# RWKV scan on one core: values repeated by DMA instead of by TensorE, and the outer mix product in four row groups

## The chip, the cores and the metric

The kernel runs on one core of one Trainium2 chip. A core has TensorE (PE, matmuls, with weight loads PEld beside them), VectorE (DVE), ScalarE (ACT), GpSimd (POOL) and SyncE (SP, which here only issues DMAs). Matmuls write to PSUM; everything else lives in SBUF, and DMA engines move data between SBUF and DRAM. The metric is device time in microseconds, the median of some runs. Before the change it is 3527.54 us (3 runs, 3523.34 to 3530.71).

## The reference

Four layers run one after the other on x of shape (16, 100, 512): a cross-attention (layer 0), an RWKV block (layer 1), a second cross-attention with a feed-forward part (layer 2), and another RWKV block (layer 3). The change touches the two RWKV blocks alone. Their core, with 32 heads of 16 channels:

```python
xa = _ln(x, ln1_w, ln1_b)
sx = jnp.concatenate([state[:, 1:2] - xa[:, :1], xa[:, :-1] - xa[:, 1:]], axis=1)
xxx = jnp.tanh((xa + sx * maa_x) @ maa_w1).reshape(b, l, 5, DM)
xxx = jnp.einsum('blfd,fde->blfe', xxx, maa_w2)
xm = xa[:, :, None] + sx[:, :, None] * (maa_stack + xxx)
xk, xw, xv, xr, xg = (xm[:, :, j] for j in range(5))
w = jnp.exp(-jnp.exp(time_decay + jnp.tanh(xw @ td_w1) @ td_w2)).reshape(b, l, h, s_)
r, k, v = (...)   # xr @ Wr.T, xk @ Wk.T, xv @ Wv.T
g = jax.nn.silu(xg @ Wg.T)
def step(s, rkvw):
    r_t, k_t, v_t, w_t = rkvw
    a = k_t[..., :, None] * v_t[..., None, :]
    out = jnp.einsum('bhi,bhij->bhj', r_t, u * a + s)
    s = a + w_t[..., :, None] * s
    return (s, out)
```

For each head the state is a 16 x 16 matrix: every key channel i meets every value channel j. Behind the recurrence stand a group norm, the gate, the product with Wo, and a channel mix with three more 512 x 512 products (Wfk, Wfr, Wfv). The mix product is the second einsum: five mixes f, each a product over only DM = 32 hidden channels into 512 output channels.

## The kernel before

The 16 sequences are worked in 4 groups g of 4 (T = 400 columns: 4 sequences of 100 steps), and the 512 channels in 4 chunks c of 128. A chunk C = 4g + c holds 8 heads, that is 8 x 256 pairs (i, j), which lie on 128 partitions x 2 rows in 8 *units*. An RWKV layer has 16 chunks and so 128 units; the loop at L1231 runs over them, from u = -42 (group 0's projections come first, with no units) to a tail behind unit 127. DVE, ACT, POOL and PE instructions that go through the wrappers at L69 and L81 keep the order in which the program writes them (their line in the profile is L77 or L82); SP's DMAs do not go through a wrapper.

What one slot u of the loop writes (L1251 to L1274):

- `spread(u + 1)`: two matmuls of 32 rows each, one for each row of a unit's row pair, with a 0/1 matrix `sel`, repeat the value rows of the chunk (`vc`) over 128 partitions into a PSUM tile `vb` (two of them in turn, two banks each), shifted by one step; ACT copies the start state from `s0r` into each sequence's first column.
- `product(u)`: DVE multiplies `vb` by the repeated keys `kr`, in place, 128 x 792.
- what was put off to this slot: readers of PSUM banks of the slot before (`slots.begin()`), among them `tm` on DVE and `xj` on POOL for the mixes.
- `scan(u)`: two DVE scans (128 x 400 each) over the decay `wr` and `vb`, into an SBUF tile `a` (4 of them); then POOL multiplies `a` by the repeated receptance `rr`, in place.
- `enter`, `repeat`, `bonus`, `gates` at fixed slots of a chunk: DMAs on SP that load a chunk's v, k, r (`vc`, `kc`, `rc`) and the repeated `kr`, `wr`, `rr` (one tile for two rows; four DMAs each, one for a quarter of the partitions) from DRAM, where `store` put them from ACT's queue.
- `gather` in odd slots: PE sums the finished units u-3 and u-2 over i into the PSUM bank `acc`; after a chunk's last one comes `norm`.
- then *pieces*: projections of the next group, the product with Wo, the channel mix. Each has a price in us, and a slot takes pieces until a budget is used up: 2.5 in units 0 to 28, 2.95 up to unit 95, 3.9 from unit 96 on, less what gather and bonus take.

The mix product is `mixed(f, c)`, twenty pieces of 0.67 in a group, each one matmul of 32 rows into a bank of its own; three banks `mm0` to `mm2` serve all pieces. Every group: 2 inner products (`inner`), then mixes, keys (`plain` with Wk), decay, values, receptance and gate in the order written out at L945 to L969.

The core of a unit, in the code:

```python
vector.tensor_tensor_scan(
    a[:, i, :], rep["w"][:, i, :], vbs[u % 2][:, i, :T], 0.0, ALU.mult, ALU.add
)
gpsimd.tensor_tensor(a, a, rep["r"], ALU.mult)
```

Of the kernel before, what the change touches and what calls it, by code (L numbers as in the profile page):

```python
# [9 lines left out]
F32 = mybir.dt.float32  # L10
# [7 lines left out]
G = 4  # L18
# [17 lines left out]
def xattn_sequence(ctx: ExitStack, tc: tile.TileContext, d: dict, out: bass.AP):  # L36
# [42 lines left out]
    vector, scalar, gpsimd = InOrder(nc.vector), InOrder(nc.scalar), InOrder(nc.gpsimd)  # L79
# [80 lines left out]
    class Slots:  # L160
# [22 lines left out]
        def read_later(self, bank, fn):  # L183
            once = self.readers[id(bank)] = self.defer(1, fn)
            return once
# [450 lines left out]
    def rwkv(n, ws, next_weights, last):  # L636
# [6 lines left out]
        with ExitStack() as es:  # L643
# [6 lines left out]
            vbs = [psum.tile([128, 2, 512], F32, name=f"vb{i}") for i in range(2)]  # L650
            acc = psum.tile([128, 512], F32, name="acc")
            slots = Slots([psum.tile([128, 512], F32, name=f"mm{i}") for i in range(3)])
# [3 lines left out]
            w2a = one.tile([128, E], F32, name="maa_w2a")  # L656
            nc.sync.dma_start(out=w2a, in_=d[f"L{n}_maa_w2"][0:128, :])

            w2b = one.tile([96, E], F32, name="td_maa_w2")
            nc.sync.dma_start(out=w2b[:64], in_=d[f"L{n}_td_w2"])  # L660
            nc.sync.dma_start(out=w2b[64:], in_=d[f"L{n}_maa_w2"][128:160, :])
# [27 lines left out]
            fold = one.tile([128, 32], F32, name="fold")  # L689
            nc.vector.tensor_reduce(fold, ident.rearrange("p (r s) -> p s r", s=32), AX.X, ALU.add)  # L690
            sel = one.tile([128, 16, 32], F32, name="sel")
            for j in range(16):
                nc.vector.tensor_copy(
                    sel[:, j, :].rearrange("p (h i) -> p h i", i=16),
                    fold.rearrange("p (h j) -> p h j", j=16)[:, :, j : j + 1].to_broadcast([128, 2, 16]),
                )


            share = one.tile([128, 2], F32, name="share")
            nc.vector.tensor_reduce(share, heads8.rearrange("p (q h) -> p h q", h=2), AX.X, ALU.add)  # L700
# [3 lines left out]
            for jg in range(4):  # L704
                nc.vector.tensor_copy(
                    gat[:, jg, :].rearrange("p (h g q) -> p g q h", g=4, q=4)[:, jg],
                    heads8.rearrange("p (q h) -> p q h", h=2),
                )
                nc.vector.tensor_tensor(
                    gat[:, jg, :].rearrange("p (h j) -> p h j", j=16),  # L710
                    gat[:, jg, :].rearrange("p (h j) -> p h j", j=16),
                    share[:, :, None].to_broadcast([128, 2, 16]), ALU.add,
                )

            s0r = one.tile([128, 4, NC, 4, B], F32, name="s0r")
            for r in range(4):
                rs = slice(32 * r, 32 * r + 32)
                ps = slots.bank()
                for c in range(NC):
                    for jq in range(4):  # L720
                        mm(
                            out=ps[32 * jq : 32 * jq + 32, c * 64 : (c + 1) * 64], lhsT=ident[rs, rs],
                            rhs=s0[rs, c].rearrange("p b (g q) -> p q g b", q=4)[:, jq],
                            start=True, stop=True,
                        )
# [72 lines left out]

            def projections(g, base):
                nm = f"{n}_{g}"  # L800
                to = put[g] = {
                    t: dram.tile([NC, 4, 32, T], F32, tag=t, name=f"d{t}_{nm}")
                    for t in ("k", "v", "r", "w", "g")
                }

                def store(t, c, tile):
                    nc.scalar.dma_start(out=to[t][c].rearrange("r p t -> (r p) t"), in_=tile)
# [48 lines left out]
                def inner(lo, hi):  # L856
                    p0, z = (0, "z0") if lo == 0 else (64, "tz")
                    rs = slice(p0, p0 + hi - lo)
                    chain(
                        2.7, late, None, soon, lambda ps: ps[rs, :T], lambda c: w1[:, c, lo:hi],  # L860
                        lambda c: st["xm"][:, c, :],
                        lambda ps: scalar.activation(st[z][rs, :], ps[rs, :T], AF.Tanh),
                    )

                def mixed(f, c):

                    if c == 0:
                        xj[f] = two.tile([128, NC, T], F32, tag="xm", bufs=3, name=f"xj_{nm}_{f}")
                    ps = slots.bank()
                    cols = slice(c * 128, (c + 1) * 128)  # L870
                    rs = slice(32 * f, 32 * f + 32) if f < 4 else slice(64, 96)
                    w, z = (w2a, st["z0"]) if f < 4 else (w2b, st["tz"])
                    mm(out=ps[:, :T], lhsT=w[rs, cols], rhs=z[rs, :], start=True, stop=True)

                    def read():
# [6 lines left out]
                    mixes[f].append(slots.read_later(ps, read))  # L882
# [61 lines left out]
                mix = lambda f, c: piece(0.67, lambda: mixed(f, c), late)  # L944
                inner(0, 128)  # L945
                mix(0, 0)
                inner(128, 160)
                for c in range(1, NC):
                    mix(0, c)
                mix(1, 0)  # L950
                mix(1, 1)
                plain(0, "Wk", "k", 0)
                plain(0, "Wk", "k", 1)
                mix(1, 2)
                plain(0, "Wk", "k", 2)
                mix(1, 3)
                plain(0, "Wk", "k", 3)
                mix(2, 0)
                decay_in()
                for c in range(NC):  # L960
                    if c:
                        mix(2, c)
                    piece(0.67, lambda c=c: decay(c), late)
                for f, w, t in ((2, "Wv", "v"), (3, "Wr", "r")):
                    for c in range(NC):
                        mix(f + 1, c)
# [4 lines left out]
            def channels(g, slot):  # L971
# [41 lines left out]
                def keys(co):  # L1013
                    def read(ps):
                        if co == 0:
                            st["kk"] = two.tile([128, NC, T], F32, tag="kk", bufs=1, name=f"kk_{nm}")
# [19 lines left out]
                def values(i):  # L1036
                    b = g * G + i

                    def read(ps):
                        def add():  # L1040
# [3 lines left out]
                            if last:  # L1044
                                nc.sync.dma_start(out=out[b], in_=xb[b])
# [43 lines left out]
            def enter(C):  # L1089
# [4 lines left out]
                for k, bufs in (("v", 2), ("k", 1), ("r", 1)):  # L1094
                    t[k] = two.tile([128, T], F32, tag=f"{k}c", bufs=bufs, name=f"{k}c_{n}_{C}")
                    nc.sync.dma_start(out=t[k], in_=put[g][k][c].rearrange("r p t -> (r p) t"))
                repeat(C, 0)

            def repeat(C, rp):
                g, c = C // NC, C % NC  # L1100
                rep = chunks[C]["rep"][rp] = {}
                for t in ("k", "w", "r"):
                    rep[t] = two.tile([128, 2, T], F32, tag=f"{t}rep", bufs=3, name=f"{t}r_{n}_{C}_{rp}")
                    for jq in range(4):
                        nc.sync.dma_start(
                            out=rep[t][32 * jq : 32 * jq + 32],
                            in_=put[g][t][c, 2 * rp : 2 * rp + 2].rearrange("r p t -> p r t"),
                        )
# [23 lines left out]
            def spread(u):  # L1132

                C, jg, rp = where(u)
                p4 = vbs[u % 2][:, :, :T].rearrange("p r (b t) -> p r b t", t=L)
                for i in range(2):
                    rs = slice(64 * rp + 32 * i, 64 * rp + 32 * i + 32)
                    mm(
                        out=p4[:, i, :, 1:L], lhsT=sel[rs, 4 * jg : 4 * jg + 4, :].rearrange("p q m -> p (q m)"),
                        rhs=steps(chunks[C]["v"][rs, :])[:, :, 0 : L - 1], start=True, stop=True,  # L1140
                    )
                g = C // NC
                scalar.copy(
                    p4[:, :, :, 0], s0r[:, 2 * rp : 2 * rp + 2, C % NC, jg, g * G : (g + 1) * G]
# [577 lines left out]
```

## Time and profile before

| | us |
|---|---|
| median of 3 runs | 3527.54 |
| the profiled execution | 3530.07 |
| its span, first to last instruction | 3528.3 |
| layer 1: units 0 to 28 | 859 to 987 |
| layer 1: units 29 to 63 | 987 to 1147 |
| layer 1: units 64 to 95 | 1147 to 1313 |
| layer 1: units 96 to 127 | 1313 to 1499 and a little on |
| layer 3: the same four | 2785, 2913, 3072, 3238, 3425 |
| spread on PE (`vb<-vc,sel`), both layers | 261.0 |
| mix product on PE (`mm<-z,maa_w2a`, f under 4), both layers | 120.2 |
| POOL's `a<-a,rr`, 256 times | 480.9 |
| DVE's scans, 512 times | 475.7 |
| DVE's product, 256 times | 250.5 |

Busy time is the union of a group's instructions[...]. A float32 matmul stands in the profile as two records. The share of the TensorE clock that was granted is 0.935 over the span. Idle time of an engine that does not set the pace costs nothing. DMAs are issued from SP (queue q1) and ACT (q10).

### The profile page before, as it was taken

How to read it: one execution, taken by the hardware profiler on the slowest of the kernel's cores; microseconds unless marked ns; L12 is line 12 of the kernel's file. 1: busy time of each engine (PE TensorE's matmuls, PEld its weight loads, DVE VectorE, ACT ScalarE, POOL GpSimd, SP SyncE). 2: the span in 40 equal slices, each digit the busy share in tenths (PEclk: the TensorE clock that was granted, in tenths of full speed). 3: DMA queues.
4: the chain of work that ended last, by engine and by line, in shares of the span. 5: the costliest groups of instructions: out<-in, count | busy, mean ns of one | idle time of the engine just before them, and what ended most of it. 6: DMA issues, size and time to landing. Idle time of an engine off the chain costs nothing. (4 is left out here: it accounts for less than half of the span.)

```text
span 3528.3 us, 46276 instructions
## 1 busy us (share of the span) xinstructions
PE 3217.1 (91%) x17795; PEld 1432.9 (41%) x17795; DVE 1770.8 (50%) x3570; ACT 981.8 (28%) x1715; POOL 1376.4 (39%) x1036
## 2 busy tenths in 40 slices
PE   6899998868999988988999999789998899998898
PEld 3444443333333333334454555345553333333333
DVE  4777777723777665514333333310001477775651
ACT  1322223222233233321322223211112233333232
POOL 1444444443666665511212111210002466665551
PEclk8999999978999989999999999999997899998998
DMA  5000001012434441101000010110012243433310
GB/s 169 21 31 21 31 21 33 1 56 86 126 108 124 126 146 54 38 27 55 25 19 19 19 31 18 39 53 8 10 57 68 87 129 104 134 115 117 87 29 14
DMA packets 153426, 216.60 MB, mean 61 GB/s; under 512 B 23498, under 2 KB 132106, under 8 KB 153206
## 3 DMA queue, kind: packets, MB, share of 16 engines
q1 hardware_dynamic: 130166, 180.87, 17.3%
q10 hardware_dynamic: 23040, 32.78, 2.6%
q8 instruction: 140, 2.29, 0.3%
q14 instruction: 80, 0.66, 0.1%
HBM read 174.25 MB, written 36.04 MB: 60 GB/s over the span
## 5 line engine op out<-in xcount | busy, mean ns | idle before, releaser
L77 POOL TENSOR_TENSOR a<-a,rr 128x800 f32<-128x800 f32 x256 | 480.9, 1879 | 342.4 <-DVE a L77 269.7
L77 DVE TENSOR_TENSOR_SCAN a<-wr,vb 128x400 f32<-128x400 f32 x512 | 475.7, 971 | 19.8 <-PE acc L82 10.9
L77 DVE TENSOR_TENSOR vb<-vb,kr 128x792 f32<-128x792 f32 x256 | 250.5, 979 | 197.0 <-ACT vb L77 195.5
L77 DVE CUSTOM_DVE_ANT_0 junk<-l_sc,mask 100x361 f32<-100x361 f32 x512 | 273.0, 533 | 90.1 <-PE l_sc L82 73.6
L82 PE MATMUL vb<-vc,sel 32*128 32x396 f32 x1024 | 261.0, 568 | 3.4 <-DVE a L77 2.2
L77 DVE TENSOR_TENSOR pt<-l_sc,maskT 121x400 f32<-121x400 f32 x384 | 193.5, 566 | 89.9 <-PE l_sc L82 89.0
L77 ACT ACTIVATE pt<-pt 121x1600 f32<-121x1600 f32 x96 | 147.6, 1538 | 282.2 <-DVE pt L77 280.7
L1425 DVE CUSTOM_DVE_ANT_0 junk<-l2a_sc,mask 100x361 f32<-100x361 f32 x256 | 136.9, 535 | 172.9 <-PE l2a_sc L82 155.7
L77 POOL TENSOR_TENSOR xj<-tm,ext 128x400 f32<-128x400 f32 x160 | 152.8, 962 | 174.3 <-DVE tm L77 168.0
L77 DVE SCALAR_TENSOR_TENSOR tm<-mm,vec,sx 128x400 f32<-128x400 f32 x160 | 99.9, 631 | 235.6 <-PE mm L82 190.9
L1461 POOL TENSOR_TENSOR pa<-pt,pt 121x1600 f32<-121x1600 f32 x16 | 57.2, 3574 | 366.8 <-ACT pt L1456 366.8
L63 PE MATMUL h<-yTb,l_fc 128*128 128x400 f32 x512 | 175.3, 505 | 8.2 <-ACT yTb L229 8.2
L1642 DVE TENSOR_TENSOR x<-pb,x 100x512 f32<-100x512 f32 x16 | 12.8, 799 | 338.3 <-DMA pb<-po 332.7
L82 PE MATMUL v<-l_v_w,ct 128*121 128x512 f32 x384 | 180.0, 613 | 0.0
L82 PE MATMUL k<-ct,l_k_w 128*128 128x361 f32 x512 | 173.0, 481 | 7.3 <-DVE mv_l2a L207 7.3
L77 POOL TENSOR_TENSOR pa<-pt,pt 121x1600 f32<-121x1600 f32 x32 | 114.7, 3586 | 165.5 <-ACT pt L77 165.5
L63 PE MATMUL p<-l_proj,h 128*128 128x512 f32 x384 | 165.4, 592 | 0.0
L77 ACT COPY vb<-s0r 128x8 f32<-128x8 f32 x256 | 43.0, 168 | 408.7 <-PE vb L82 322.9
L82 PE MATMUL l_sc<-kz,qz 32*100 32x361 f32 x1024 | 117.1, 528 | 42.6 <-DVE pt L77 21.7
L82 PEld LDWEIGHTS vb<-vc,sel 32*128 32x128 f32 x1024 | 84.8, 190 | 146.9 <-issue 107.3
L82 PE MATMUL mm<-l_Wo,gc 128*100 128x512 f32 x256 | 124.6, 629 | 8.4 <-POOL gc L77 8.4
L63 PEld LDWEIGHTS h<-yTb,l_fc 128*128 128x128 f32 x512 | 98.1, 192 | 83.3 <-ACT yTb L229 10.1
(258 smaller groups left out, 5305.6 us busy)
## 6 DMA issues: line engine op xcount, KB each, us to landing
kr<-dk SPq DMA_DIRECT2D x256, 100.0 KB
wr<-dw SPq DMA_DIRECT2D x256, 100.0 KB
rr<-dr SPq DMA_DIRECT2D x256, 100.0 KB
ct<-in_ctxT SPq DMA_DIRECT2D x32, 722.0 KB
dk<-k ACTq DMA_DIRECT2D x32, 200.0 KB
kc<-dk SPq DMA_DIRECT2D x32, 200.0 KB
dw<-wd ACTq DMA_DIRECT2D x32, 200.0 KB
dv<-v ACTq DMA_DIRECT2D x32, 200.0 KB
```

What stands on the lines that cost most here:

```text
L63: nc.tensor.matmul(out=ps, lhsT=lhs(c), rhs=rhs(c), start=(c == 0), stop=(c == n - 1))
L77: return lambda *args, **kw: tc.keep_in_program_order(op(*args, **kw))
L82: pin(nc.tensor.matmul(**kw))
L1425: nc.vector.tensor_tensor_reduce(out=junk, in0=ss[r][:L, :S2], in1=t["mask"], scale=-1.0, scalar=FLT_MAX, op0=ALU.add, op1=ALU.min, accum_ ...
L1461: nc.gpsimd.tensor_tensor(t["pa"], t["pt"][0], pt, ALU.add)
L1642: nc.vector.tensor_tensor(x, pb[:, i, :], x, ALU.add)
```

## The change

Values are no longer spread by PE. The stores of k, v, r and w in DRAM get another order (channel by channel, so that the four rows of a partition stand beside each other), the values one element further on, with a small number in front, so that a read from the element before gives the values shifted by one step. `fetch(u)` then brings a unit's values, repeated, straight into its tile `a` (now 6 tiles), with two DMAs of 64 partitions, two slots ahead. ACT writes the first column there (`first`), product and scans work in place in `a`. The repeats of k, w and r become one DMA of 128 partitions each, spread over more slots, and the stores and the loads of v, k and r become four DMAs each. The matrices `gat`, `fold` follow the new order of the partitions. SP's DMAs in this part are now kept in program order too.

The PSUM of `vb` goes to the pieces, which have seven banks instead of three. `hidden(f)` copies the 32 rows of a mix's hidden channels to all four quarters of the partitions (four DMAs on SP), the weights `w2a` lie by chunks in the four quarters, and `mixed(f)` writes the four chunks' matmuls one after the other, each in its own rows of PE and its own bank. It is one piece of 0.75. Its readers come one slot later for c = 0, 1 and two for c = 2, 3. The order of the pieces is written anew. The budgets stay. Further, the weights of the channel mix are loaded in quarters over slots 82 to 96 instead of at once in slot 93, and the tile `kk` shares its buffers with the mixes.

```diff
-            vbs = [psum.tile([128, 2, 512], F32, name=f"vb{i}") for i in range(2)]
-            slots = Slots([psum.tile([128, 512], F32, name=f"mm{i}") for i in range(3)])
+            slots = Slots([psum.tile([128, 512], F32, name=f"mm{i}") for i in range(7)])
...
-            w2a = one.tile([128, E], F32, name="maa_w2a")
-            nc.sync.dma_start(out=w2a, in_=d[f"L{n}_maa_w2"][0:128, :])
+            w2a = one.tile([128, 5, 128], F32, name="maa_w2a")
+            for c in range(NC):
+                nc.sync.dma_start(
+                    out=w2a[32 * c : 32 * c + 32],
+                    in_=d[f"L{n}_maa_w2"][:, c * 128 : (c + 1) * 128].rearrange("(f k) m -> k f m", k=32),
+                )
...
                 def store(t, c, tile):
-                    nc.scalar.dma_start(out=to[t][c].rearrange("r p t -> (r p) t"), in_=tile)
+                    for ps, rows in rows_of(g, t, c):
+                        nc.scalar.dma_start(out=rows, in_=tile[ps])
...
+                def hidden(f):
+                    z = st["z0"][32 * f : 32 * f + 32, :] if f < 4 else st["tz"][64:96, :]
+                    t = st["zr", f] = two.tile([128, T], F32, tag="zr", bufs=2, name=f"zr_{nm}_{f}")
+                    for c in range(NC):
+                        sync.dma_start(out=t[32 * c : 32 * c + 32, :], in_=z)
+                def mixed(f):
+                    xj[f] = two.tile([128, NC, T], F32, tag="xm", bufs=3, name=f"xj_{nm}_{f}")
+                    banks = [slots.bank() for c in range(NC)]
+                    for c, ps in enumerate(banks):
+                        rs = slice(32 * c, 32 * c + 32)
+                        mm(out=ps[:, :T], lhsT=w2a[rs, f, :], rhs=st["zr", f][rs, :], start=True, stop=True)
+                    if f < 4:
+                        hidden(f + 1)
...
+                    for c, ps in enumerate(banks):
+                        mixes[f].append(slots.read_later(ps, lambda c=c: read(c), 1 + c // 2))
...
                 inner(0, 128)
-                mix(0, 0)
                 inner(128, 160)
+                mix(0)
+                plain(0, "Wk", "k", 0)
+                mix(1)
...
-            def spread(u):
+            def fetch(u):
                 C, jg, rp = where(u)
-                p4 = vbs[u % 2][:, :, :T].rearrange("p r (b t) -> p r b t", t=L)
-                for i in range(2):
-                    rs = slice(64 * rp + 32 * i, 64 * rp + 32 * i + 32)
-                    mm(
-                        out=p4[:, i, :, 1:L], lhsT=sel[rs, 4 * jg : 4 * jg + 4, :].rearrange("p q m -> p (q m)"),
-                        rhs=steps(chunks[C]["v"][rs, :])[:, :, 0 : L - 1], start=True, stop=True,
-                    )
+                g, c = C // NC, C % NC
+                a = products[u] = two.tile([128, 2, T], F32, tag="a", bufs=6, name=f"a_{n}_{u}")
+                v = put[g]["v"]
+                for h in range(2):
+                    n0 = v.offset + (c * 128 + 64 * h + 16 * jg + 2 * rp) * T
+                    sync.dma_start(
+                        out=a[64 * h : 64 * h + 64],
+                        in_=bass.AP(v.tensor, n0, [[0, 16], [4 * T, 4], [1, 2 * T]]),
+                    )
+            def first(u):
...
                 scalar.copy(
-                    p4[:, :, :, 0], s0r[:, 2 * rp : 2 * rp + 2, C % NC, jg, g * G : (g + 1) * G]
+                    products[u].rearrange("p r (b t) -> p r b t", t=L)[:, :, :, 0],
+                    s0r[:, 2 * rp : 2 * rp + 2, C % NC, jg, g * G : (g + 1) * G],
                 )
...
             def product(u):
                 C, jg, rp = where(u)
-                p4 = vbs[u % 2][:, :, :T].rearrange("p r (b t) -> p r b t", t=L)
+                p4 = products[u].rearrange("p r (b t) -> p r b t", t=L)
...
-                a = products[u] = two.tile([128, 2, T], F32, tag="a", bufs=4, name=f"a_{n}_{u}")
+                a = products[u]
                 for i in range(2):
-                    vector.tensor_tensor_scan(
-                        a[:, i, :], rep["w"][:, i, :], vbs[u % 2][:, i, :T], 0.0, ALU.mult, ALU.add
-                    )
+                    vector.tensor_tensor_scan(a[:, i, :], rep["w"][:, i, :], a[:, i, :], 0.0, ALU.mult, ALU.add)
                 gpsimd.tensor_tensor(a, a, rep["r"], ALU.mult)
...
                     rep[t] = two.tile([128, 2, T], F32, tag=f"{t}rep", bufs=3, name=f"{t}r_{n}_{C}_{rp}")
-                    for jq in range(4):
-                        nc.sync.dma_start(
-                            out=rep[t][32 * jq : 32 * jq + 32],
-                            in_=put[g][t][c, 2 * rp : 2 * rp + 2].rearrange("r p t -> p r t"),
-                        )
+                    x = put[g][t]
+                    n0 = x.offset + (c * 128 + 2 * rp) * T
+                    sync.dma_start(
+                        out=rep[t], in_=bass.AP(x.tensor, n0, [[4 * T, 32], [0, 4], [1, 2 * T]])
+                    )
...
-                if u == UNITS - 32 - 3:
-                    cm.update(load(n, "Wfk", "Wfr", "Wfv"))
+                for k, at_u in (("Wfk", UNITS - 46), ("Wfr", UNITS - 40), ("Wfv", UNITS - 35)):
+                    if 0 <= u - at_u < NC:
+                        load_part(cm, n, k, u - at_u)
...
+                if 0 <= u + 2 < UNITS:
+                    fetch(u + 2)
                 if 0 <= u + 1 < UNITS:
-                    spread(u + 1)
+                    first(u + 1)
```

## The prediction

> **What bounds the kernel now.** The page's first part says that TensorE is 91% busy and that no other engine passes 50%. That is an average, so I went on to the busy time by stage. The product instruction of a unit (one slice of the RWKV recurrence) writes `vb` once; its start times in the timeline cut each RWKV layer into units. The stretches below hold layer 1's units 0-29, 29-64, 64-96 and 96-127 (layer 3 repeats them within 1 us; the two layers' units are 1280 of 3528 us). Columns: length, then busy us (instructions) of PE, weight load, DVE, ACT, POOL, then granted clock, DMA share, GB/s.
> ```profile
> PE 3217.1 (91%) x17795; PEld 1432.9 (41%) x17795; DVE 1770.8 (50%) x3570; ACT 981.8 (28%) x1715; POOL 1376.4 (39%) x1036
> ...
> 859.00:987.00 128.00, 125.43 (x460) 47.67 (x458) 97.41 (x121) 36.60 (x83) 86.11 (x70) 0.92 0.35 103
> 987.00:1147.00 160.00, 152.29 (x596) 58.22 (x596) 118.01 (x148) 57.40 (x118) 106.53 (x86) 0.94 0.39 115
> 1147.00:1313.00 166.00, 149.80 (x557) 56.91 (x557) 110.01 (x137) 54.86 (x110) 110.16 (x94) 0.90 0.45 136
> 1313.00:1499.00 186.00, 173.76 (x594) 63.26 (x592) 110.45 (x133) 64.68 (x127) 98.27 (x79) 0.92 0.18 51
> ```
> A unit lasts 128/29 = 4.41, 4.57, 5.19 and 6.00 us, and TensorE fills 90 to 98% of it. DVE and POOL have room, but only as long as they may run at the same time: their busy times add up to 183.5 us in a stretch of 128. So the next question is what lets them overlap. The groups and the per-tile views show whom:
> ```profile
> L77 POOL TENSOR_TENSOR a<-a,rr x256: 1861/1878/1901, 869.2 to 3431.3; 128x800 f32<-128x800 f32 x128
> ...
> L77 DVE TENSOR_TENSOR_SCAN a<-wr,vb x512: 954/969/989, 867.3 to 3430.1; 128x400 f32<-128x400 f32 x171
> L77 DVE TENSOR_TENSOR vb<-vb,kr x256: 958/980/992, 859.4 to 3424.5; 128x792 f32<-128x792 f32 x128
> ...
> L77 DVE SCALAR_TENSOR_TENSOR th_1b<-th_1b,mm x16: 653/689/689, 1340.6 to 1597.3; 100x512 f32<-100x512 f32 x16
> L77 DVE SCALAR_TENSOR_TENSOR x<-th_1b,x x16: 691/692/1650, 1341.4 to 1598.0; 100x512 f32<-100x512 f32 x16
> ...
> L1642 DVE TENSOR_TENSOR x<-pb,x x16: 691/693/1751, 2369.1 to 2668.5; 100x512 f32<-100x512 f32 x16
> ```
> (Three numbers: shortest/median/longest ns.) The product and the scans each read one operand from PSUM (`vb`), and neither they nor POOL's multiplication ever stretch, though they run beside each other all the time. The two DVE instructions with both inputs in SBUF, `x<-th_1b,x` and `x<-pb,x`, take 0.69 us or up to 1.75. The timeline shows when they stretch:
> ```profile
> 1438.80 0.69 DVE L77 SCALAR_TENSOR_TENSOR th_1b<-th_1b,mm 100x512 f32<-100x512 f32 x1 [1.61 <-PE mm L82]
> 1439.53 1.30 DVE L77 SCALAR_TENSOR_TENSOR x<-th_1b,x 100x512 f32<-100x512 f32 x1
> ...
> 1439.25 1.04 POOL L77 TENSOR_TENSOR og<-og,sq 128x400 f32<-128x400 f32 x1 [0.89 <-ACT sq L77]
> ...
> 1470.23 1.88 POOL L77 TENSOR_TENSOR a<-a,rr 128x800 f32<-128x800 f32 x1
> 1470.28 0.69 DVE L77 SCALAR_TENSOR_TENSOR th_1b<-th_1b,mm 100x512 f32<-100x512 f32 x1 [2.56 <-PE mm L82]
> 1471.01 1.65 DVE L77 SCALAR_TENSOR_TENSOR x<-th_1b,x 100x512 f32<-100x512 f32 x1
> ```
> POOL's `og` ends at 1440.29 and the DVE instruction at 1440.83; POOL's `a` ends at 1472.11, DVE at 1472.66: each time 0.55 us later, its 0.69 without a start-up. It stood still until POOL was done. `th_1b<-th_1b,mm`, same length, one operand in PSUM, ran through the same POOL instruction in 0.69. The reverse shows too: a `gc` multiplication that POOL started at 1351.85 behind a DVE instruction of two SBUF inputs took 1.48 us, not 1.03, and ended 0.89 after it.
>
> [...] The trace agrees in every such pair of full length (above; beside `rstd`, of 4 elements, nothing stretched). No scan with two SBUF inputs is in it[...]. [...] layer 0's `l_sc<-qz,kz` (768 records, two a matmul, four row groups in turn) has 92.8 us, 0.24 a matmul, against 120.2/128 = 0.94 for the mix product's `mm<-z,maa_w2a`.
>
> **The change, part by part** (profiled execution: 3530.07 us, span 3528.28).
>
> 1. *Spread removed from PE.* 512 matmuls, 261.0 us of PE over both layers: 1.02 us of each unit. A gain only where PE stays the bound.
> 2. *Mix product side by side.* 20 matmuls a group become 5 bursts: 20 x 0.87 to 0.94 less 5 x 0.97, some 13 us of PE a group, 0.4 a unit. In group 0's lead-in (745-859, no scans, PE 94.6 of 114 busy) this lies on the path; against it stands the first `zr` copy, which now sits between tanh and mix (bounds 0 and 5 us, estimated from four SP issues at 0.4 each and the landing; the 1.7 to 3 us of the second inner product cover part). I take -8 a layer, between -14 and 0.
> 3. *Product and scans read SBUF twice.* `a` now comes by DMA, so product (`a`, `kr`) and scans (`wr`, `a`) have no PSUM operand left. By the lock, all of POOL's SBUF work and these three instructions stand in one line. No gain in their own length: `x<-th_1b,x` and `th_1b<-th_1b,mm` show 691 and 689 ns. Two bounds for a layer:
>    - *Upper*: whole intervals. Product to scan 1.06 and two scans 1.78 (starts 1442.53, 1443.59; 1440.75, 1442.53) = 2.84 a unit, plus all of POOL's busy time. 29 units: 82.4 + 86.1 = 168.5 for 128.0 now, +40. Then 99.4 + 106.5 for 160, +46; 90.9 + 110.2 for 166, +35; 88.0 + 98.3 + 5.5 (eight `x<-th`) for 186, +6. Sum +127.
>    - *Lower*: an instruction that was blocked has its start-up behind it. Estimates from the stretched pairs: product 0.85 (792 at 1.07 ns), each scan 0.85, 2.55 a unit; 0.14 less for each POOL instruction (1.03 to 0.89). 74.0 + 76.3 for 128.0, +22; 89.3 + 94.5, +24; 81.6 + 97.0, +13; 79.1 + 87.2 + 4.4, -15. Sum +43.
>    The middle, +85 a layer, +170 for both. In units 96-127 PE would need 174 - 32 = 142, under either sum, so the lock is the bound there as well.
> 4. *DMA.* A unit fetches 128 x 3200 B = 0.41 MB; with `k`, `w`, `r` repeats (6 x 0.41), loads and stores (1.8 MB) each chunk of 8 units moves 7.6 MB, 0.95 a unit. At 5.5 us that is 170 GB/s. Now queue 1 moves 180.87 MB in 17.3% of 16 engines' span, which makes 296 GB/s at full use: 58%. Cost nothing, hidden under six buffers of `a` (fetched two units ahead); at 3.6 us a unit it would be 89% and no longer free.
> 5. *Queues.* SP issues about 40 DMAs a chunk, 5 a unit at 0.37 to 0.43 us: 2.1 us of 5.5. It is now kept in order: behind a fetch that waits for the gather of six units earlier stand the repeats and `zr` copies; that gather runs about two units before its buffer is asked for. ACT issues 4 stores for 1, 48 more a group at 0.33: 0.5 a unit on top of 1.3 to 2.1 busy. Behind a late fetch ACT's column copy (0.17) would hold up tanh and copies. Both nothing in the sum; in the upper bound I put 30 us a layer.
> 6. Set-up, the weights split in quarters, the shared `kk` buffer (its ring gives out three tiles a group, each free before its successor): nothing.
>
> Sum: 3530 + 170 - 16 = 3684 profiled; the median of the runs stands 2.5 lower, and I round to **3680**. Own range of this case: 3530 + 86 - 28 = 3588 to 3530 + 254 + 60 = 3844.
>
> **Rivals.** (a) *[...] POOL slips in between* (the other sign): the trace has no such scan, and only the product would then block. The place is the scan's first operand; it decides once the lock sum falls under the PE time of now (4.4 to 6 a unit). Then DVE sets 3.6 a unit (3.37 busy now): 104 for 128, 126 for 160, 120 for 166, and PE 154 for 186: -136 a layer, 3530 - 272 - 16 = 3242, say 3250. For it: PE's 91%; against it: the pairs above. (b) *The fetch is the bound*: if 0.95 MB goes at half of 296 GB/s, a unit takes 6.4 us; (2.0 x 29 + 1.8 x 35 + 1.2 x 32 + 0.4 x 31) = 172 a layer, 3860.[...] (c) *Balance*: the lower sum, with the lead-in and tail gaining more than I give them: 3530. (d) That the changed code doesn't do what it says I see no sign of.
>
> **How the numbers follow.** Lock 0.78, (a) 0.15, (b) 0.04, (c) 0.03. Range 3530 to 3830: left out are (a), and some 0.05 above. 0.2% (7 us) is about what a measurement of this kernel tells from no change: faster 0.15, same 0.03, slower 0.82.
>
> **What would show it.** Right: product, scans and `a<-a,rr` no longer have fixed lengths (some 1.8 us longer at worst), a unit of 5.2 to 5.9 us up to unit 96, DVE near full while PE falls to about 60%, and the two never streaming at once. `mm<-z` at about 1 us for four. Wrong: 0.97 and 1.88 us throughout, units under 4.4 us; or DVE idle with DMA named as releaser of ACT's column copy.

## The result, and the profile after

3779.32 us (median of four runs, 3773.99 to 3790.96), against 3526.94 for the kernel before, run beside it: ratio 1.072, 95% interval 1.0692 to 1.0748. The change makes the kernel 7% slower; 3680 was predicted, with a range to 3830. The profiled execution took 3790.96 us, its span 3789.2, that is 260.9 more than the span before.

The page of the kernel after: first the busy times, then its costliest groups. Columns of a group: busy us and mean ns of one, then the idle time of the engine just before them and what ended most of it.
```profile
PE 3053.1 (81%) x16771; PEld 1415.2 (37%) x16771; DVE 2143.3 (57%) x3548; ACT 977.0 (26%) x1715; POOL 1653.7 (44%) x1038
...
L77 DVE TENSOR_TENSOR_SCAN a<-wr,a 128x400 f32<-128x400 f32 x512 | 793.0, 1588 | 153.9 <-ACT a L77 143.4
L77 POOL TENSOR_TENSOR a<-a,rr 128x800 f32<-128x800 f32 x256 | 582.0, 2274 | 360.6 <-DVE a L77 85.3
...
L77 DVE TENSOR_TENSOR a<-a,kr 128x792 f32<-128x792 f32 x256 | 321.1, 1254 | 3.2 <-DMA a<-dv 3.1
...
L82 PE MATMUL mm<-rk,ones 128*128 128x400 f32 x64 | 52.7, 925 | 249.5 <-POOL rk L77 249.5
...
L77 ACT COPY a<-s0r 128x8 f32<-128x8 f32 x256 | 49.8, 201 | 449.2 <-DMA a<-dv 223.2
```
PE's busy time fell by 164 us (3217.1 to 3053.1). By groups, spreading and mixing take 365 us less, but other work on PE takes longer, above all the gathers (`acc<-a,gat`, 158.6 us for 125.4) and the start state, of which more below. DVE gained 372 and POOL 277, though neither got more to compute: their instructions became longer. The scans went from 475.7 us to 793.0, the product from 250.5 to 321.1, POOL's multiplication from 480.9 to 582.0. Shortest, median and longest of these, in the view of the tile `a`:
```profile
L77 DVE TENSOR_TENSOR_SCAN a<-wr,a x512: 956/1580/3779, 876.1 to 3695.9; 128x400 f32<-128x400 f32 x171
L77 DVE TENSOR_TENSOR a<-a,kr x256: 949/953/3783, 865.9 to 3692.5; 128x792 f32<-128x792 f32 x128
...
L77 POOL TENSOR_TENSOR a<-a,rr x256: 1860/2382/3162, 882.6 to 3697.2; 128x800 f32<-128x800 f32 x128
```
The shortest are what they were before (954, 958, 1861 ns). So the operations themselves cost the same from SBUF; the rest is standing still. The timeline shows at what (start, length, engine; in brackets the idle time before it):
```profile
1102.37 2.56 POOL L77 TENSOR_TENSOR a<-a,rr 128x800 f32<-128x800 f32 x1
1103.18 2.60 DVE L77 TENSOR_TENSOR_SCAN a<-wr,a 128x400 f32<-128x400 f32 x1
...
1105.70 0.95 DVE L77 TENSOR_TENSOR a<-a,kr 128x792 f32<-128x792 f32 x1
1106.00 2.38 POOL L77 TENSOR_TENSOR a<-a,rr 128x800 f32<-128x800 f32 x1 [1.07 <-DMA dk<-k]
1106.75 4.15 DVE L77 TENSOR_TENSOR_SCAN a<-wr,a 128x400 f32<-128x400 f32 x2
...
1108.35 1.71 POOL L77 TENSOR_TENSOR gc<-gc,og 128x400 f32<-128x400 f32 x1
```
POOL's first multiplication ends at 1104.93; the scan that started beside it ends 0.85 later, at 1105.78. The product ends at 1106.65, POOL's next multiplication 1.73 later, at 1108.38. `gc` ends at 1110.06, 1.68 after that, which leaves 0.83 for itself if the first scan took its 0.85 in between; the second scan ends at 1110.90, 0.84 after `gc`. Each instruction begins its stream where the other engine's ends, and needs its own length less 0.1 to 0.2. Here the two engines stream one after the other, without a gap and never together: this is what is called the lock below and in the prediction.

By stage, layer 1's lead-in and the units 0-29, 29-64, 64-96 and 96-127 (columns as in the prediction):
```profile
745.00:866.00 121.00, 95.05 (x344) 60.31 (x344) 22.88 (x62) 23.13 (x43) 29.91 (x42) 0.77 0.30 85
866.00:1044.00 178.00, 112.32 (x374) 43.44 (x374) 144.12 (x124) 43.98 (x95) 121.37 (x78) 0.75 0.55 160
1044.00:1249.00 205.00, 128.14 (x442) 52.38 (x442) 177.51 (x147) 55.53 (x115) 146.62 (x88) 0.76 0.56 167
1249.00:1450.00 201.00, 127.58 (x429) 50.18 (x428) 156.91 (x137) 54.36 (x110) 141.90 (x89) 0.78 0.58 172
1450.00:1641.00 191.00, 158.11 (x482) 59.29 (x482) 143.73 (x135) 63.66 (x128) 133.34 (x81) 0.86 0.43 126
```
A unit now takes 6.14, 5.84, 6.28 and 6.18 us, from the start times of the products, against 4.41, 4.58, 5.18 and 6.00. PE fills 63% of the first three stages; DVE fills 78 to 87%. The units of layer 1 take 135 us more, those of layer 3 136. Outside the units little moved: layer 1's first unit starts 6.5 us later, the time between the two layers' units is 10 shorter, the tail 7 shorter. 135 + 136 + 6.5 - 10 - 7 = 260.5, which is the difference of the spans.

How much of the 135 is the line of DVE and POOL? I took the union of the intervals in which POOL, one of DVE's three instructions or `x<-th` runs: 5.43, 5.34, 5.54 and 5.72 us a unit. Set against the old length of a unit, (5.43 - 4.41) x 29 + (5.34 - 4.58) x 35 + (5.54 - 5.18) x 32 + (5.72 - 6.00) x 31 = +59 a layer. What is left, 0.71, 0.50, 0.74 and 0.46 us a unit or some 76 a layer, is time in which nothing of the line moves. This divides the time; it does not yet say what causes either part. DVE's gaps there end with ACT's copy into the column of `a` (0.26, 0.49, 0.94 and 0.53 a unit) and PE's bank (0.86, 0.21, 0.26, 0.92). So there were two questions for the runs: is the line itself what it looks like, and what are the waits on top of it?

### The profile page after: what moved, and what is told of

Its sections match the earlier page's. It is cut to its first block, busy times and chain, and to the rows that moved or that the text cites. A ratio compares the mean times of both kernels' runs of the same rounds, so it can differ in the third digit from the quotient of the medians.

```text
span 3789.2 us, 45867 instructions
## 1 busy us (share of the span) xinstructions
PE 3053.1 (81%) x16771; PEld 1415.2 (37%) x16771; DVE 2143.3 (57%) x3548; ACT 977.0 (26%) x1715; POOL 1653.7 (44%) x1038
## 5 line engine op out<-in xcount | busy, mean ns | idle before, releaser
L77 DVE TENSOR_TENSOR_SCAN a<-wr,a 128x400 f32<-128x400 f32 x512 | 793.0, 1588 | 153.9 <-ACT a L77 143.4
L77 POOL TENSOR_TENSOR a<-a,rr 128x800 f32<-128x800 f32 x256 | 582.0, 2274 | 360.6 <-DVE a L77 85.3
L77 DVE TENSOR_TENSOR a<-a,kr 128x792 f32<-128x792 f32 x256 | 321.1, 1254 | 3.2 <-DMA a<-dv 3.1
L77 POOL TENSOR_TENSOR xj<-tm,ext 128x400 f32<-128x400 f32 x160 | 218.9, 1391 | 94.0 <-DVE tm L77 94.0
L82 PE MATMUL mm<-rk,ones 128*128 128x400 f32 x64 | 52.7, 925 | 249.5 <-POOL rk L77 249.5
L82 PE MATMUL acc<-a,gat 128*32 128x400 f32 x1024 | 158.6, 606 | 64.3 <-POOL a L77 64.1
L77 ACT COPY a<-s0r 128x8 f32<-128x8 f32 x256 | 49.8, 201 | 449.2 <-DMA a<-dv 223.2
L82 PE MATMUL mm<-xj,l_Wk 128*128 128x400 f32 x256 | 109.3, 571 | 36.0 <-POOL xj L77 35.8
L77 POOL TENSOR_TENSOR pa<-pa,pt 119x1600 f32<-119x1600 f32 x32 | 114.5, 3578 | 43.1 <-ACT pt L77 42.9
```

The lines of the kernel that those rows point to most:

```text
L77: return lambda *args, **kw: tc.keep_in_program_order(op(*args, **kw))
L82: pin(nc.tensor.matmul(**kw))
```

## The experiments

All medians below are from a comparison with runs of the kernel before beside them, at 3526.9 to 3529 us.

**e1: the kernel before, with the scan's operand in SBUF.** PE still spreads the values; the product reads PSUM and writes SBUF, and the scans work there.
```diff
                 vector.tensor_tensor(
-                    p4[:, :, :, 1:L], p4[:, :, :, 1:L],
+                    products[u].rearrange("p r (b t) -> p r b t", t=L)[:, :, :, 1:L], p4[:, :, :, 1:L],
...
-                        a[:, i, :], rep["w"][:, i, :], vbs[u % 2][:, i, :T], 0.0, ALU.mult, ALU.add
+                        a[:, i, :], rep["w"][:, i, :], a[:, i, :], 0.0, ALU.mult, ALU.add
...
```


> The kernel before, values still spread by TensorE into PSUM; only the product's result goes to the SBUF tile a, and the scans work in place there, so that they have two SBUF inputs (the product has one). Lock theory: scans and POOL exclude each other, scans stretch to 1.3 us and more on the mean (0.97 before), a unit up to unit 64 takes 4.7 to 5.2 us (4.41 and 4.58 before), the time is 3560 to 3640. Rival (a late fetch by DMA is what costs, the scan takes no lock): nothing of that is in this kernel, so scans 0.97 and 3527 within 10 us.

Measured: 3646.18 (3642.47 to 3648.86), ratio 1.0336 (1.032 to 1.0351). View of the tile `a`:
```profile
L77 DVE TENSOR_TENSOR_SCAN a<-wr,a x512: 956/1396/3129, 867.8 to 3543.1; 128x400 f32<-128x400 f32 x171
...
L77 DVE TENSOR_TENSOR a<-vb,kr x256: 948/951/984, 859.6 to 3537.3; 128x792 f32<-128x792 f32 x128
```
No DMA and no piece was moved (ACT's column copy goes to `a` too, and `kk` shares the mixes' buffers, as in e4, which is faster), and the scans stretch; the product beside them, with one operand in PSUM, never does. The lock on the scan is shown, and it alone takes some 119 us in a kernel that PE otherwise bounds, nearly all of it in the units (58 and 62).

That this is twice the 59 of the union above is a coincidence. In e1 POOL and the scans together fill 4.50, 4.63, 5.00 and 4.87 us of layer 1's units, at most 0.09 more than the old length of a unit, and the units take 4.94, 5.07, 5.68 and 6.30, of which PE fills 86 to 92%. So the lock costs time although neither its line nor PE is full, and although no queue got more to do.

**e2: the kernel after, with the product in PSUM again.** One PSUM tile of two banks was taken from the pieces for it; the scans read that.
```diff
-            slots = Slots([psum.tile([128, 512], F32, name=f"mm{i}") for i in range(7)])
+            vb = psum.tile([128, 2, 512], F32, name="vb")
+            slots = Slots([psum.tile([128, 512], F32, name=f"mm{i}") for i in range(5)])
...
-                    vector.tensor_tensor_scan(a[:, i, :], rep["w"][:, i, :], a[:, i, :], 0.0, ALU.mult, ALU.add)
+                    vector.tensor_tensor_scan(a[:, i, :], rep["w"][:, i, :], vb[:, i, :T], 0.0, ALU.mult, ALU.add)
...
-                if 0 <= u + 1 < UNITS:
-                    first(u + 1)
                 if unit:
+                    first(u)
                     product(u)
```


> The changed kernel, values by DMA as there; only the product writes to PSUM (two banks, so five remain for the pieces) and the scans read it there. Lock theory: scans are back at 0.97 us, only the product and POOL exclude each other, a unit takes 4.0 to 4.6 us up to unit 96 and about 5.2 after, the time is 3300 to 3450. Rival (the fetch sets the pace): units stay at about 6 us, 3700 to 3790.

Measured: 3862.96 (3851.31 to 3865.63), ratio 1.0945 (1.0927 to 1.0962), slower than the change itself. View of the tile `vb`, then DVE's longest wait:
```profile
L77 DVE TENSOR_TENSOR_SCAN a<-wr,vb x512: 951/966/989, 883.8 to 3768.5; 128x400 f32<-128x400 f32 x171
...
L77 DVE TENSOR_TENSOR vb<-a,kr x256: 991/2563/2720, 882.4 to 3764.8; 128x792 f32<-128x792 f32 x128
```
```profile
DVE vb L77 <- ACT vb L77: 447.1, 234, 17.5
```
The scans are free again, but the experiment brought in three costs of its own. With a single tile, ACT can write the next column only after the scans, and the product waits for it 234 times. And since the product, still with two SBUF inputs, now always starts when POOL has just begun the unit's multiplication, nearly every one stands still for it (median 2563 ns). And with five banks for the pieces layer 1's units start 16.5 us later than in the kernel after, and the stretch between the two layers' units is 18.6 longer. It says nothing on the size of the lock; e7 is its repair.

**e3: the kernel after, with the values fetched three units ahead** (seven tiles `a`; one `gc` and one staging buffer fewer to make room).
```diff
-                if 0 <= u + 2 < UNITS:
-                    fetch(u + 2)
+                if 0 <= u + 3 < UNITS:
+                    fetch(u + 3)
```


> The changed kernel with seven tiles a and the fetch three slots ahead instead of two (one tile less for gates and for staging, to make room). Lock theory: DVE's waits for the first column (143 us over both layers) mostly go, but the line of DVE and POOL stays: units 5.7 to 5.9 up to 64, the time is 3700 to 3770. Rival (a late fetch sets the pace): 3400 to 3550.

Measured: 3783.75 (3782.51 to 3786.8), ratio 1.0728 (1.0712 to 1.0744); units of 6.13, 5.84, 6.31 and 6.18 us, as in the kernel after. The order did come earlier (14.7 us ahead of the product in the median unit of layer 1, for 10.4), and ACT's waits for the values fell from 223 to 126 us; but DVE's waits for ACT's column stayed at 142 us (143 in the kernel after), against the expectation. How early the values are ordered doesn't set the time of the changed kernel. Their rate this run can't tell; e8 can, where the same bytes go through in shorter units.

**e4: the mix product alone, on the kernel before.** Its three `mm` banks allow two chunks side by side, so the four go in two pairs; PE spreads the values as before, `kk` shares the mixes' buffers.
```diff
-                def mixed(f, c):
+                def mixed(f, h):
...
+                    banks = {c: slots.bank() for c in (2 * h, 2 * h + 1)}
+                    for c, ps in banks.items():
+                        rs = slice(32 * c, 32 * c + 32)
+                        mm(out=ps[:, :T], lhsT=w2a[rs, f, :], rhs=st["zr", f][rs, :], start=True, stop=True)
+                    if h == 0 and f < 4:
+                        hidden(f + 1)
```


> The kernel before, values spread by TensorE into PSUM; only the mix product changes: two chunks side by side in two row groups (three banks are free), with the copies of the hidden channels by DMA. If TensorE bounds the units, 20 matmuls of 0.87 us a group become 10 pairs of about 0.9: 8 us a group, 34 a layer, the time is 3455 to 3480. Rival (the mix product isn't on the path, or the copy's wait eats it): 3515 to 3560.

Measured: 3486.39 (3481.49 to 3491.69), ratio 0.9879 (0.9862 to 0.9895), the fastest of all here. The groups of the kernel after and of e4, from the groups by shape:
```profile
L82 PE MATMUL mm<-zr,maa_w2a 32*128 32x400 f32 x320 | 57.8, 565 | 11.8 <-ACT ew L77 10.3 <-DMA zr<-z 1.6
```
```profile
L82 PE MATMUL mm<-zr,maa_w2a 32*128 32x400 f32 x320 | 86.6, 580 | 4.3 <-DVE tm L77 3.5 <-ACT ew L77 0.5
```
320 records are 160 matmuls: 0.36 us of PE each in fours, 0.54 in pairs, 0.94 before (120.2/128). This half of the change is a gain even in pairs, and by itself it makes the kernel 1.2% faster. Of the 38.4 us between the spans 3.5 lie ahead of layer 1's units, 17.6 between the two layers' units, 6.0 in the tail and only 11.3 in the units. The new order of the pieces is part of this version and wasn't tried apart.

**e6 and e9: the `zr` copies issued from ACT instead of SP**, in the kernel after (e6) and in e4 (e9).
```diff
                     for c in range(NC):
-                        sync.dma_start(out=t[32 * c : 32 * c + 32, :], in_=z)
+                        scalar.dma_start(out=t[32 * c : 32 * c + 32, :], in_=z)
```


> The changed kernel, only the zr copies are issued from ACT's queue, behind the tanh that they wait for, and no longer stand in SP's line in front of the fetches (SP waited some 20 us there three times in layer 1). If that wait is what the time holds above the line of DVE and POOL (5.4 of 6.1, 5.3 of 5.8, 5.6 of 6.3 and 5.7 of 6.2 us a unit), units fall to 5.5 to 5.9 and the time to 3650 to 3740. If the line alone sets the pace and the waits only fill in, 3765 to 3790.

> The kernel before with the mix product in pairs (values still spread by TensorE), and the zr copies from ACT's queue instead of SP's. SP has slack there and isn't kept in order, so little: within 15 us of the run with pairs (3486). If the copies' issues on ACT delay its reads of PSUM, slower by 10 to 20 us.

Measured: e6 3767.44 (3760.23 to 3771.98), ratio 1.0677 (1.0658 to 1.0695); e9 3490.04 (3484.2 to 3492.8), ratio 0.9895 (0.988 to 0.991). In the kernel after, SP stood at these copies for some 61 us of layer 1's first three stages, with the fetches behind it. Taking it away gave 12 us in all, where the two intervals still touch: nearly the whole wait had been covered. In e4 it gave nothing.

**e7: e6 with the product in two PSUM tiles, as before the change.** The columns are written a slot ahead again; three banks are left for the pieces, so the mix goes in pairs.
```diff
-            slots = Slots([psum.tile([128, 512], F32, name=f"mm{i}") for i in range(7)])
+            vbs = [psum.tile([128, 2, 512], F32, name=f"vb{i}") for i in range(2)]
+            slots = Slots([psum.tile([128, 512], F32, name=f"mm{i}") for i in range(3)])
...
-                    vector.tensor_tensor_scan(a[:, i, :], rep["w"][:, i, :], a[:, i, :], 0.0, ALU.mult, ALU.add)
+                    vector.tensor_tensor_scan(a[:, i, :], rep["w"][:, i, :], vbs[u % 2][:, i, :T], 0.0, ALU.mult, ALU.add)
...
```


> As the run with zr from ACT, and the product writes to PSUM (two tiles in turn, as the kernel before had them), the scans read there, ACT's column goes there a slot ahead, and the mix product is done in pairs, since three banks are left. Lock theory: only the product and POOL exclude each other, scans 0.97 us, units 3.9 to 4.5 up to 96 and about 5.2 after, the time is 3320 to 3450. Rival (queues and fetches set the pace whatever the lock does): 3600 and more.

Measured: 3632.07 (3624.25 to 3643.58), ratio 1.0302 (1.0279 to 1.0326). View of the tile `vb`, and DVE's wait for it:
```profile
L77 DVE TENSOR_TENSOR_SCAN a<-wr,vb x512: 951/966/989, 878.1 to 3528.7; 128x400 f32<-128x400 f32 x171
...
L77 DVE TENSOR_TENSOR vb<-a,kr x256: 956/993/2691, 876.6 to 3526.4; 128x792 f32<-128x792 f32 x128
```
```profile
DVE vb L77 <- ACT vb L77: 260.1, 73, 11.9
```
With the scans out of the line, 135 us of e6's time are gone. In the units of the two profiled executions it is 171; some 24 are lost again ahead of them, in a version that has three banks for the pieces and mixes in pairs. So the lock on the scans is the largest single cost found. But the theory asked for 3320 to 3450, and 104 us over the kernel before are left (by the profiled executions 94, of which 82 in the units), although PE has no spreading to do and the scans don't stretch. The lock is the first cost, and there is a second.

**e8: e6 without POOL's multiplication by the receptance.**
```diff
-                gpsimd.tensor_tensor(a, a, rep["r"], ALU.mult)
```


> As the run with zr from ACT, and POOL's multiplication of a by rr is left out (the recurrence's output is then the sum of the states without r), which takes 1.74 us a unit out of the line of DVE and POOL and changes no DMA and no DVE work. Lock theory: units fall by 1.2 to 1.7 us, to 4.2 to 4.7 up to 96, the time is 3350 to 3480. Rival (queues and fetches): no more than 60 us below the run with zr from ACT.

Measured: 3541.33 (3538.75 to 3552.48), ratio 1.0049 (1.003 to 1.0068); units of 5.11, 4.83, 5.30 and 5.49 us. 226 us less than e6, or 0.88 a unit for an instruction of 1.88. A line without holes that alone sets the pace would give back its whole stream of 1.73 a unit, at least up to unit 96. It doesn't, and a kernel that still fetches everything but has neither spreading on PE nor 481 us of POOL's work is still no faster than the one before.

**e10 and e11: the column's copy on DVE instead of ACT**, in e7 (e10) and in e8 (e11). In e7 and e8 the wait ahead of the product or the scan was mostly for this copy, and it stands on ACT behind the orders for DMA. In the kernel after, ACT's timeline reads:
```profile
901.59 1.74 ACTq L820 DMA_DIRECT2D dk<-k  x4
903.37 0.21 ACT L77 COPY a<-s0r 128x8 f32<-128x8 f32 x1 [1.81 <-DMA dk<-k]
```
Four orders take 1.74 us of ACT, and a copy of 0.21 goes behind them.
```diff
             def first(u):
...
-                scalar.copy(
+                vector.tensor_copy(
```


> As e7 (product to PSUM, scans from PSUM, copies of the mix's rows issued from ACT), with one change: the small copy that writes a unit's state columns runs on DVE, just ahead of the product before it, and not on ACT. In e7 DVE waited about 260 us for that copy, which stood on ACT behind four stores to DRAM a piece and the copies' issues. Theory (ACT's queue of DMA issues delays the column, and DVE behind it): the waits for the column go, DVE pays 256 small copies of about 0.1 to 0.2 us (26 to 50 us), and the sum falls to 3440 to 3570. Rival (the wait only changes its name: DVE waits for PE's mm bank, for the transfer of the values or for ACT's reads instead): 3600 or more.

> As e8 (without POOL's multiplication of the scan's result by the receptance, so the output leaves out r; product and scans in SBUF), with the state column's copy on DVE instead of ACT. e8 took 3541. Theory (what was left over in e8 is ACT's queue): 3400 to 3490. Rival (what was left is shared out over several queues, or the rest of DVE's work sets it): 3520 or more.

Measured: e10 3615.01 (3609.34 to 3622.02), ratio 1.0245 (1.0217 to 1.0273); e11 3537.51 (3522.28 to 3550.53), ratio 1.0025 (1.0013 to 1.0036). The groups of e10, then of e11:
```profile
L77 DVE TENSOR_TENSOR vb<-a,kr 128x792 f32<-128x792 f32 x256 | 349.9, 1367 | 106.3 <-DMA a<-dv 94.8
```
```profile
L77 DVE COPY a<-s0r 128x8 f32<-128x8 f32 x256 | 73.9, 289 | 199.7 <-DMA a<-dv 193.5
```
The 260 us for ACT are gone and the time fell by 17 in e10; in e11 by 4, which the intervals don't tell from nothing. (DVE had waited 195.5 us for this copy in the kernel before as well, with PE as the bound: such a wait is not all loss.) The wait took another name: part of it is now for the values themselves, which SP orders. That was the rival's case in both.

**e12 and e13: e10 and e11 with the values fetched three units ahead**, by the edit of e3.

> As e10 (3615 us), with the values' transfer ordered three units ahead instead of two (seven buffers for the product instead of six; one buffer less for the gate's chunk and for the staging tiles). In e10 DVE waited 95 us for the values in the two layers, and SP, which orders them, stood in line behind twelve orders for the next chunk's rows. Theory (what is left after the lock is SP's line, two units deep): the wait for the values goes, 3480 to 3580. Rival (the rest is not the fetch but PE's and POOL's turn-taking, or DVE's own queue): 3595 or more.

> As e11 (without the multiplication by the receptance, so the output leaves out r; the state column's copy on DVE; 3538 us), with the values ordered three units ahead. In e11 DVE waited 194 us for the values' transfer, 71 times. Theory (the line on SP is what is left when POOL's part of the lock is gone): 3380 to 3480, clearly under the kernel before. Rival (the copies' rate or the buffer's release holds the transfers, however early they are ordered): 3500 or more.

Measured: e12 3607.49 (3599.72 to 3623.73), ratio 1.0238 (1.0211 to 1.0265); e13 3535.35 (3523.35 to 3545.61), ratio 1.0021 (1.0012 to 1.0029). The page of e12, then of e13:
```profile
L77 DVE TENSOR_TENSOR vb<-a,kr 128x792 f32<-128x792 f32 x256 | 354.2, 1383 | 36.5 <-DMA kr<-dk 21.6
```
```profile
L77 DVE COPY a<-s0r 128x8 f32<-128x8 f32 x256 | 73.7, 288 | 113.0 <-DMA a<-dv 107.7
```
The wait for the values is nearly gone in e12 and nearly halved in e13, and the time moved by 8 and by 2 us, in both less than the intervals can tell. The times are those of the rivals. But e13's rival named the copies' rate or the release of a buffer, and the trace shows the orders themselves late: before DVE's 27 waits of over 1 us for values, the order had ended only 2.4 to 5.8 us before DVE went on, where the median unit has its order 12.0 us ahead of its product. 22 of the 27 fall on the first two units of a chunk, whose orders stand on SP behind the twelve loads of that chunk's rows, three units ahead too.

**What stays open.** In e12 a unit of the second and third stage still takes 4.92 and 4.97 us, of which PE, DVE and POOL fill 3.8 to 3.9, 3.8 to 3.9 and 3.55 each, and POOL together with the product 3.85 and 3.82. None is full. That points to turn-taking between queues that are kept in program order as the second cost, but no run gave that order up, so it is argued and not shown. One place of it that no run took away is PE's list of waits, before and after:
```profile
PE mm L82 <- POOL rk L77: 17.2, 8, 4.1
```
```profile
PE mm L82 <- POOL rk L77: 249.5, 30, 16.5
```
Once a chunk, PE's matmul `mm<-rk,ones` stands for POOL's product `rk`, in chunks 1 to 11 of layer 1 of the kernel after 10.1 us on average and 0.3 before; in e12 it is 4.7, in e13 6.1. All of PE's later pieces stand behind it, and so do the gathers, which free the tiles `a` for the next values. Part of it reaches DVE: in e12 DVE waits 101.7 us, 25 times, for the result of this matmul, in the kernel before 16.0, 12 times. PE has time to spare there, so how much of that reaches the end isn't known; it wasn't tried.

## Why the prediction was right, and where its sum was not

The sign and the mechanism held; the size was 99 us short (3680 against 3779). By its own steps:

- **Step 1**, the spread from PE: as stated. PE falls to 63% in three stages and its gain buys nothing there.
- **Step 2**, -16 for the lead-ins: mixing gave more. From the first transpose of a lead-in to the end of its last projection PE takes 76.3 us in layer 1 and 77.5 in layer 3, where it took 91.7 and 92.1, so 15 a layer, just past the bound of 14. A burst of four takes 0.95 us at best (at 913.25), as expected, and 1.45 on average (57.8/40). That the mix product would also be worth 40 us on its own, 27 of them outside the units, I hadn't worked out.
- **Step 3**, the line of DVE and POOL: 43 to 127 a layer, 85 taken. That a scan would stand still was my assumption: the trace of before shows it for `x<-th_1b,x` and `x<-pb,x` (up to 1650 and 1751 ns for 691), and has no scan with two SBUF inputs. The runs show it for the scan too (e1: 1396 ns as the median instead of 969). By the union it came to 59 a layer. The lower way of summing was nearer (5.18, 5.25, 5.58 and 5.51 us a unit, against 5.43, 5.34, 5.54 and 5.72), because an instruction that stood still ends 0.1 to 0.2 us less than its own length after the other engine's, in the timeline above, as that bound had it.
- **Step 4**, DMA for nothing: right in the changed kernel. To order earlier moves nothing (e3), and the same bytes go through faster in e8: up to unit 96, 180, 202 and 210 GB/s, where the kernel after moves 160, 167 and 172, near the 170 worked out.
- **Step 5**, queues for nothing: this is the term that was mis-sized most. Some 76 us a layer lie in gaps on top of the line, where the sum had 0 and its upper bound 30. The cost it names did come: four stores of 0.43 us in front of the column's copy, SP at the `zr` copies, orders on SP at 0.54 to 0.6 us instead of 0.37 to 0.43. But it can't be laid on one of these. Three of the waits were taken away (SP's for the `zr` copies in e6, DVE's for the column in e10, and most of its wait for the values in e12), and the time fell by 12, 17 and 8 us; the four stores themselves and the longer orders were in every version of the changed kernel. What failed is the method: each queue was costed as its busy time, hidden while it stays under the length of a unit. As I read it, with every engine's list kept in program order, and DVE and POOL handing over to each other two or three times a unit, a delay on any list becomes a hole in the line. e1 has such a loss without any new queue work, so a part of the 76 can be the lock's own.
- **Step 6**, set-up for nothing: wrong by 22 us a layer. With the new order of the partitions the start state is spread by other matmuls, with `fold`. The groups of the kernel before, then of the kernel after:
```profile
L82 PE MATMUL mm<-s,ident 32*32 32x64 f32 x256 | 5.7, 290 | 25.1 <-DMA s<-in_s 14.2 <-POOL shift_a L77 10.8
```
```profile
L82 PE MATMUL mm<-s,fold 32*128 32x64 f32 x256 | 50.4, 403 | 25.8 <-DMA s<-in_s 25.8
```
They stand ahead of everything else in each lead-in and take 25.2 us of it instead of 2.9. With the 15 that mixing gave, this is why layer 1's lead-in became 6.5 longer instead of 8 shorter. All versions of the changed kernel carry it; e1, e4 and e9 don't.

The -10.5 measured outside the units is thus near the -16 by luck: 30 gained by mixing, 45 lost by the start state, and some 25 gained elsewhere, which I didn't trace. With 59 for step 3 and 76 for step 5, 2 x 135 - 10.5 gives the 260 us between the spans. It is luck too that the miss is no larger: the line was taken 26 a layer too long, the waits 76 too short.

The signs came out mixed. The lengths of the scans, the product and `a<-a,rr` do vary, by up to 2.8 us, and PE falls to 63%. But two of the three stages have units above 5.9 us, DVE is not near full, and a sign of being wrong is there as well: DVE stands 143 us for ACT's column copy, which in turn stands 223 us for the values. e3 and e1 answer it: earlier orders don't shorten the time, and the lock costs time without any fetch.

Of the rivals, (a), that the scan takes no lock, is refuted by e1. Its sum has a slip, which decides nothing: 32 units of 3.6 us are 115 and not 120, and PE's part of the last stage is 142 in step 3 and 154 here; with the smaller ones it comes to about 3210. (b), the fetch as the bound, would give nearly the measured size (3860), but it supposed 148 GB/s, and the units of e8 are up to 1 us shorter with the same fetches. (c), a balance at 3530, would have needed the line at its lowest and no holes; e11 and e13 come out there only with POOL's multiplication left out.

## What to carry to other kernels

Before an operand moves from PSUM to SBUF to relieve PE, count the SBUF inputs of every DVE instruction that then reads it, and add POOL's time to those with two: e1 makes the same arithmetic 3.4% slower by the place of one operand (median scan 1396 ns for 969). Such a sum is no upper bound either: in e1 the line hardly passes the old length of a unit. Cost the set-up that a new layout needs as well; here it took 45 us. Where a change has two parts, price them one at a time: the mix product with its new order of pieces is 1.2% faster, and the whole change 7% slower. And where several lists in program order share a short cycle, a wait that was taken away here mostly came back under another name (260 us of waits for 17 us of time in e10), so a sum over the waits is no bound on the gain.

## What the runs showed of the hardware

- The scan with two SBUF inputs is held up like the product: 3779 ns at worst for 969, the product 3783 for 980. That scan started at 1040.41, stood while POOL's `a<-a,rr` ran to 1042.35 and then its `og<-og,sq` to 1043.34, and ended at 1044.19, 0.85 after. So a waiting DVE instruction isn't always the next to go: here POOL took two turns.
- A DVE instruction with one SBUF input was held up too. The column's copy into SBUF takes up to 1158 ns (e11), and into PSUM at most 171 (e10):
```profile
L77 DVE COPY a<-s0r x256: 142/175/1158, 869.1 to 3444.3; 128x8 f32<-128x8 f32 x128
```
```profile
L77 DVE COPY vb<-s0r x256: 153/170/171, 870.5 to 3504.3; 128x8 f32<-128x8 f32 x128
```
In e11 53 of the 256 take over 250 ns, and each of these ends within 0.15 us after an instruction of POOL that it ran beside; none of the other 203 ran wholly inside one. So to count inputs, as above, is not enough for a copy from SBUF to SBUF.
- An instruction that wasn't held up took about the same from SBUF as from PSUM: shortest product and scan from SBUF 949 and 956 ns, from PSUM 958 and 954.
- In the units the granted clock was lower where PE's work had holes: 0.90 to 0.94 before, where PE is 90 to 98% busy, 0.75 to 0.78 after at 63%, and 0.86 in the last stage after at 83%. The busy share alone doesn't give it: in the first 745 us of the kernel after PE is 86% busy at a clock of 0.94.
- An order on SP for a unit's values or for a whole repeat took 0.54 to 0.55 us at the median and one for a `zr` copy 0.59, where one for a quarter of a repeat had taken 0.42; a load of a quarter of a chunk's v, k or r took 0.42, for the whole one 0.37 to 0.42. On ACT a store of a quarter took 0.43 and a whole one 0.33, so four cost about five times as much.
